# Softmax sums of two 16-head attentions as accumulator outputs of the exponentials

## The chip, the cores and the metric

The kernel runs on one core of a Trainium2 chip. The metric is the device time of one execution in microseconds (us), measured on that core. Engines are named as in the profile: PE is TensorE (matmuls and transposes, with its weight loads as PEld), DVE is VectorE, ACT is ScalarE, POOL is GpSimd, SP is SyncE, which issues the DMAs. Each engine works through its own queue of instructions in order; semaphores hold an instruction until others have finished.

## What is computed

The reference is a chain of four layers on x (2 x 1024 tokens, 256 wide) with a context of 77 tokens. Each layer adds an attention to the context and then a feed-forward. The change touches the attentions of layers 0 and 1, which have the same form (cut from the reference):

```python
q, k, v = heads(layernorm(x) @ Wq), heads(ctx @ Wk), heads(ctx @ Wv)   # 16 heads of 16
scores = q @ k.T / 4                       # 1024 x 77 for each head
scores = where(mask, -huge, scores)
attn = softmax(scores, axis=-1)            # exp(s - max) / sum(exp(s - max))
x = x + (attn @ v) @ Wo + bo
```

The feed-forward of layer 0 is a mixture of 8 experts with all experts computed and two gated; layer 1's is an 8-bit quantized product; layer 2 has a one-head attention and a mixture of experts, layer 3 an attention with rotary embedding and a routed mixture of experts.

## The kernel before

The 2048 tokens are four groups (g) of 512; a group is four tiles (j) of 128 tokens, so an attention has 16 iterations `it = 4 g + j`. `attention(...)` (L296) is used for layer 0 (`layer0_attention`, L482) and layer 1 (`layer1_attention`, L557). It first makes the keys (`kblk`) and values (`vblk`) as block matrices, and then runs a hand-written pipeline (`pipelined`, L246): at each step `ahead` (layer norm, transposing and queries of the next group: `prepare`, `queries`), `scores(it)`, two empty stages, `values` two tiles at a time, and for layer 1 the stage `beside`, which places the pieces of layer 1's feed-forward and layer 2's attention (`quantized`, L593, to `add`, L682) beside the attention.

`scores(it)` works in two chunks c of 8 heads each, so an attention has 32 chunks:

- PE writes the mask into PSUM (L394, two matmuls with an identity of bf16) and adds the scores of 8 heads (L401), in a PSUM tile of two banks from a pool of two (`pbig`); the scores have the opposite sign.
- For each half of four heads (i = 0, 1) DVE takes the four minima (L410, which are the maxima with the sign turned), and ACT makes four exponentials, one for each head, 128 rows by 77 keys, with the minimum as bias (L412). They go to the SBUF tile s.
- DVE sums s over the keys, eight heads in one instruction (L417, 616 elements a row), and takes the reciprocal (L418). POOL multiplies the chunk by it (L419).

`values(it)` transposes two tiles' weights on PE (L437), copies them out of PSUM on ACT (L443) or DVE (L445), multiplies with the values (L450), copies on ACT (L455), multiplies with Wo (L459), and DVE adds the result to x (L464).

The queries are made at L374 and leave PSUM on ACT (L379 or L383); the transposed tokens at L175 leave it on ACT (L179) and DVE (L181). The exponential of layer 3's attention is at L981, with sums at L985, which are not touched. L1002 is a copy from PSUM on ACT in layer 3.

The program is built with `tile.TileContext(nc, schedule_with_timeline_sim=True)` (L1489): a scheduler sets the order in which each engine's instructions stand, from the program text, the dependencies and the buffers of the pools. So an edit in `scores` can also reorder instructions around it. The small tile sm comes from a pool entry of four buffers ("smc"), the minima from one of six ("mxc").

POOL also has one all-reduce over partitions, L580, for layer 1's quantized weights, which the scheduler places among the first scalings of layer 0.

Of the kernel before, what the change touches and what calls it, by code (L numbers as in the profile page):

```python
# [22 lines left out]
F32 = mybir.dt.float32  # L23
# [5 lines left out]
ALU = mybir.AluOpType  # L29
AX = mybir.AxisListType  # L30
# [3 lines left out]
P = 128  # L34
# [32 lines left out]
def tile_layers(ctx: ExitStack, tc: tile.TileContext, a: dict, out: bass.AP):  # L67
    nc = tc.nc
# [5 lines left out]
    st = ctx.enter_context(tc.tile_pool(name="st", bufs=3))  # L74
# [6 lines left out]
    def pbig(name):  # L81
        return ps2.tile([P, 2, 512], F32, tag="p2", name=name)
# [148 lines left out]
    def bc(v, n):  # L231

        return v.unsqueeze(len(v.shape)).to_broadcast([*v.shape, n])
# [62 lines left out]
    def attention(lay, weights, mask, deep=5, beside=None):  # L296
# [4 lines left out]
        with tc.tile_pool(name=f"at_{lay}", bufs=2) as ap:  # L301
# [84 lines left out]
            def scores(it):  # L386
                g, j = divmod(it, J)
                n = f"{lay}{g}{j}"
                s = ap.tile([P, 2, 8, L], F32, tag="s", name=f"s_{n}", bufs=deep)
                for c in range(KC):  # L390

                    sc = pbig(f"psc_{n}{c}")[:, :, : 4 * L]
                    for i in range(2):
                        nc.tensor.matmul(  # L394
                            sc[:, i].rearrange("p (h k) -> p h k", k=L), identb,
                            mb[:, g, j, :].unsqueeze(1).to_broadcast([P, 4, L]),
                            start=True, stop=False,
                        )
                    for i in range(2):
                        rows = slice(64 * i, 64 * i + 64)  # L400
                        nc.tensor.matmul(  # L401
                            sc[:, i], qTs[g][rows, c, j * P : (j + 1) * P],
                            kblk[g // 2][rows, c, 4 * i : 4 * i + 4, :]
                            .rearrange("p h k -> p (h k)"),
                            start=False, stop=True,
                        )
                    for i in range(2):
                        sv = sc[:, i].rearrange("p (h k) -> p h k", k=L)
                        mx = st.tile([P, 4], F32, tag="mxc", name=f"mx_{n}{c}{i}", bufs=6)
                        nc.vector.tensor_reduce(mx, sv, AX.X, ALU.min)  # L410
                        for h in range(4):
                            nc.scalar.activation(  # L412
                                s[:, c, 4 * i + h, :], sv[:, h, :], AF.Exp,
                                bias=mx[:, h : h + 1], scale=-1.0,
                            )
                    sm = st.tile([P, 8], F32, tag="smc", name=f"sm_{n}{c}", bufs=4)
                    nc.vector.tensor_reduce(sm, s[:, c], AX.X, ALU.add)  # L417
                    nc.vector.reciprocal(sm, sm)  # L418
                    nc.gpsimd.tensor_tensor(s[:, c], s[:, c], bc(sm, L), ALU.mult)  # L419
                ss[it] = s  # L420
# [49 lines left out]
            def ahead(it):  # L470

                g, j = divmod(it, J)
                if g + 1 < G and j < 3:
                    begin[j](g + 1)

            stages = [ahead, scores, lambda it: None, lambda it: None, values]
            if beside:
                stages.append(beside)
# [1014 lines left out]
```

## Time and profile before

| what | value |
|---|---|
| median of 3 timed runs | 1148.5 us (1147.95 to 1149.76) |
| the profiled execution | 1150.59 us |
| its span, first to last instruction | 1148.7 us |
| mean granted PE clock in it | 0.952 |
| busy: PE, DVE, ACT, POOL | 1029.8, 719.4, 362.1, 386.3 us |
| exponentials L412, both attentions | 512, 337 ns each, 121.5 us |
| sums L417 | 64, 785 ns each, 50.3 us |
| reciprocals L418 | 64, 191 ns each, 12.2 us |
| scalings L419 on POOL | 64, 1223 ns each, 78.3 us |

The profile's page shows one execution. Its first part gives busy time by engine, its second the span in 40 slices of 28.7 us with the busy share in tenths. The chain of work that ended last is followed back from the last instruction, at each step to what released it; its shares say on which engine and line the time was spent that nothing else hid. A group of instructions is given with its line, engine, operation, tiles (out<-in), shapes and count, then busy us and mean ns of one, then the idle time of the engine just before them and who ended it. Busy time can be asked for in chosen stretches: then a line holds the stretch, its length, the busy us (with instructions) of PE, PEld, DVE, ACT and POOL, the granted PE clock, the DMA share and GB/s. The exponentials of layer 0 run from 28 to some 159 us, those of layer 1 from some 313 to 436 us.

### The profile page before, as it was taken

The numbers are of one execution on the slowest core, as the hardware profiler recorded it, in microseconds if no ns is written. First come the engines' busy times: TensorE is split into PE (matmuls) and PEld (weight loads), VectorE is DVE, ScalarE is ACT, GpSimd is POOL, SyncE is SP. The second block draws the span as 40 slices with busy tenths as digits, with TensorE's granted clock in tenths as the row PEclk, the third lists the DMA queues.
The fourth block names the chain that finished last, engine by engine and source line by source line (L and its number), as shares of the span: only waits on it lengthen the run. The fifth ranks groups of instructions, "written<-read, shape, count | busy, mean of one in ns | idle before, by whom it ended". The sixth has DMA issues, their size and how long they took to land.

```text
span 1148.7 us, 13916 instructions
## 1 busy us (share of the span) xinstructions
PE 1029.8 (90%) x4770; PEld 645.5 (56%) x4770; DVE 719.4 (63%) x1848; ACT 362.1 (32%) x1115; POOL 386.3 (34%) x368
## 2 busy tenths in 40 slices
PE   5499999999998987897998999899899958999996
PEld 3255554444444444455655546577678844766774
DVE  5567965776578898949586547677878731222211
ACT  1457640000076563131231110555355521111100
POOL 5443320112343544423120000675566641121211
PEclk9699998999999898898999999999999987999998
DMA  8400008245200000111102004523042323253630
GB/s 269 57 3 1 1 23 165 38 82 88 80 1 1 1 1 1 39 48 31 40 23 59 1 1 161 145 45 67 23 103 51 90 83 96 77 165 101 200 131 17
DMA packets 100279, 74.89 MB, mean 65 GB/s; under 512 B 57916, under 2 KB 90476, under 8 KB 100206
## 3 DMA queue, kind: packets, MB, share of 16 engines
q1 hardware_dynamic: 92974, 58.20, 18.3%
q10 hardware_dynamic: 4800, 9.46, 4.8%
q0 software_dynamic: 2432, 6.31, 1.6%
q8 instruction: 40, 0.66, 0.2%
q14 instruction: 33, 0.27, 0.1%
HBM read 55.35 MB, written 19.64 MB: 65 GB/s over the span
## 4 chain that ended last, share of the span: by engine, by line
PE 56%; DVE 24%; DMA 7%; ACT 4%; issue 4%; POOL 4%; SPq 0%; POOLq 0%; DVEq 0%; ACTq 0%
PE pe_f L545 10%; PE pgu_f L745 8%; PE poe_e L1273 4%; PE ph_e L1253 4%; PE po_a L1007 4%; DMA out_x<-ye_e,ids_e 3%; PE pq_a L930 3%; DVE x L765 3%; PE pc_a L450 3%; DVE x L156 2%; PE po_f L758 2%; PE pPT_a L437 2%; DVE mx_a L410 2%; DMA xe_e<-buf 2%; DVE sm_a L417 2%
## 5 line engine op out<-in xcount | busy, mean ns | idle before, releaser
L412 ACT ACTIVATE s_a<-psc_a,mx_a 128x77 f32<-128x77 f32 x512 | 121.5, 337 | 58.5 <-DVE mx_a L410 52.1
L419 POOL TENSOR_TENSOR s_a<-s_a,sm_a 128x616 f32<-128x616 f32 x64 | 78.3, 1223 | 123.9 <-DVE sm_a L418 89.4
L545 PE MATMUL pe_f<-ew,xnT_f 128*128 128x512 f32 x256 | 117.1, 607 | 0.0
L551 DVE SCALAR_TENSOR_TENSOR x<-pe_f,gate_f,x 128x256 f32<-128x256 f32 x128 | 61.8, 483 | 43.3 <-PE pe_f L545 40.7
L981 ACT ACTIVATE s_a<-s_a,mx_a 128x77 f32<-128x77 f32 x256 | 67.2, 347 | 61.4 <-DVE mx_a L979 61.2
L545 PEld LDWEIGHTS pe_f<-ew,xnT_f 128*128 128x128 f32 x256 | 48.3, 195 | 55.0 <-issue 53.0
L1007 PE MATMUL po_a<-vw,PT_a 128*128 128x256 f32 (+1 forms) x320 | 77.3, 381 | 0.8 <-ACT PT_a L1002 0.8
L1253 PE MATMUL ph_e<-xT_e,w 128*128 128x320 f32 x256 | 75.6, 436 | 0.0
L758 PE MATMUL po_f<-down2T,hT_f 128*128 128x256 f32 x256 | 65.0, 400 | 8.8 <-DVE x L765 8.7
L437 PE MATMUL pPT_a<-cst,s_a 128*128 128x128 f32 (+1 forms) x320 | 55.0, 292 | 17.8 <-POOL vr_a L343 11.5
L410 DVE TENSOR_REDUCE mx_a<-psc_a 128x4 f32<-128x308 f32 x128 | 57.9, 466 | 18.6 <-PE psc_a L401 11.4
L1077 DVE TENSOR_SCALAR hT_e<-ph_e,b1c 128x320 f32<-128x320 f32 (+1 forms) x36 | 20.6, 572 | 75.3 <-PE ph_e L1253 75.3
L930 PE MATMUL pq_a<-wq,xnT_a 128*128 128x512 f32 x128 | 60.5, 610 | 4.7 <-DVE s_a L972 4.7
L745 PE MATMUL pgu_f<-xnT_f,gate2T 128*128 128x512 f32 x128 | 63.5, 619 | 1.0 <-DVE hT_f L751 0.6
L765 DVE SCALAR_TENSOR_TENSOR x<-po_f,cw_f,x 128x256 f32<-128x256 f32 x128 | 60.8, 480 | 5.7 <-PE po_f L758 2.5
L437 PEld LDWEIGHTS pPT_a<-cst,s_a 128*128 128x128 f32 (+1 forms) x320 | 35.9, 143 | 49.5 <-issue 17.9
L1007 PEld LDWEIGHTS po_a<-vw,PT_a 128*128 128x128 f32 (+1 forms) x320 | 57.8, 190 | 9.6 <-issue 1.4
L1075 ACT ACTIVATE hT_e<-ph_e,b1c 128x320 f32<-128x320 f32 (+1 forms) x36 | 19.6, 545 | 138.0 <-PE ph_e L1253 138.0
L1273 PE MATMUL poe_e<-w,hT_e 128*128 128x256 f32 x256 | 61.3, 381 | 0.0
L758 PEld LDWEIGHTS po_f<-down2T,hT_f 128*128 128x128 f32 x256 | 48.3, 197 | 22.7 <-DVE x L765 15.4
L450 PE MATMUL pc_a<-PT_a,vblk_a 128*32 128x256 f32 (+1 forms) x512 | 57.2, 400 | 4.2 <-DVE PT_a L445 2.2
L745 PE MATMUL pgu_f<-xnT_f,up2T 128*128 128x512 f32 x128 | 60.1, 592 | 0.0
(311 smaller groups left out, 1979.8 us busy)
## 6 DMA issues: line engine op xcount, KB each, us to landing
w<-in_L_ffn_w SPq DMA_DIRECT2D x16, 1024.0 KB
rb_a<-in_relbias SPq DMA_DIRECT2D x16, 616.0 KB
buf<-none ACTq DMA_DIRECT2D x12, 769.5 KB
vd<-vo SPq DMA_DIRECT2D x8, 308.0 KB
vw<-vd SPq DMA_DIRECT2D x2, 1152.0 KB
xe_e<-buf SPq DMA_DIRECT2D x8, 257.0 KB
x<-in_x SPq DMA_DIRECT2D x4, 512.0 KB
ew<-in_L_ffn_expert_w SPq DMA_DIRECT2D x4, 512.0 KB
```

The costliest lines, as they stand in the source:

```text
L410: nc.vector.tensor_reduce(mx, sv, AX.X, ALU.min)
L412: nc.scalar.activation(s[:, c, 4 * i + h, :], sv[:, h, :], AF.Exp, bias=mx[:, h : h + 1], scale=-1.0,)
L437: nc.tensor.transpose(pt[: wide(m), m - m0, k * P : (k + 1) * P], sp[k][:, c, m * P : m * P + wide(m)], ident,)
L450: nc.tensor.matmul(pc[cols, c, :], vblk[g // 2][: wide(m), c, m, cols], t[: wide(m), m, :], start=(k == 0), stop=(k == 1),)
L545: nc.tensor.matmul(pe[:, i, :], xnT[:, kc, j * P : (j + 1) * P], ew[half][:, kc, i * 512 : (i + 1) * 512], start=(kc == 0), stop=(kc == KC ...
L745: nc.tensor.matmul(pgu[:, i, :], wgu[i][:, kc, e * INTER : (e + 1) * INTER], xnTs[g][:, kc, :], start=(kc == 0), stop=(kc == KC - 1),)
L758: nc.tensor.matmul(po[:, e // 2, (e % 2) * D : (e % 2) * D + D], hTs[g, half][:, e, j * P : (j + 1) * P], wd[:, 4 * half + e, :], start=Tr ...
L765: nc.vector.scalar_tensor_tensor(x, po[:, e // 2, (e % 2) * D : (e % 2) * D + D], cws[g][:, j, ee : ee + 1], x, ALU.mult, ALU.add,)
L930: nc.tensor.matmul(pq[:, i, :], xnTs[g][:, kc, j * P : (j + 1) * P], wq[:, kc, i * 512 : (i + 1) * 512], start=(kc == 0), stop=(kc == KC - 1),
L1007: nc.tensor.matmul(po, t[:w, m, :], vws[g // 2][:w, m, :], start=(m == 0), stop=(m == NC3 - 1))
L1253: nc.tensor.matmul(ph[:, h % 2, :rows], w1[:, kc, h * P : (h + 1) * P], xT[:, kc, :], start=(kc == 0), stop=(kc == KC - 1),)
L1273: nc.tensor.matmul(po, hT[:, h, i * P : (i + 1) * P], w2[:, h, :], start=(h == 0), stop=(h == NH - 1),)
```

## The change

The tile sm is taken before the exponentials. Each exponential writes the sum of its 77 results into one column of sm as its accumulator output. The DVE sum of the chunk is gone; the reciprocal and the scaling stay. Layer 3's softmax and layer 2's stay as they are. In the changed file the lines of this function from the minimum to the exponential stand one lower (L411, L413); L418 and L419 keep their numbers.

```diff
                         start=False, stop=True,
                     )
+                sm = st.tile([P, 8], F32, tag="smc", name=f"sm_{n}{c}", bufs=4)
                 for i in range(2):
                     sv = sc[:, i].rearrange("p (h k) -> p h k", k=L)
                     mx = st.tile([P, 4], F32, tag="mxc", name=f"mx_{n}{c}{i}", bufs=6)
                     nc.vector.tensor_reduce(mx, sv, AX.X, ALU.min)
                     for h in range(4):
                         nc.scalar.activation(
                             s[:, c, 4 * i + h, :], sv[:, h, :], AF.Exp,
                             bias=mx[:, h : h + 1], scale=-1.0,
+                            accum_out=sm[:, 4 * i + h : 4 * i + h + 1],
                         )
-                sm = st.tile([P, 8], F32, tag="smc", name=f"sm_{n}{c}", bufs=4)
-                nc.vector.tensor_reduce(sm, s[:, c], AX.X, ALU.add)
                 nc.vector.reciprocal(sm, sm)
                 nc.gpsimd.tensor_tensor(s[:, c], s[:, c], bc(sm, L), ALU.mult)
```

## The prediction

> **What bounds the kernel now.** I read the page's engine shares and its chain of work that ended last, then the chain again stretch by stretch, then the engines' busy time in the same stretches, and last the groups of instructions with their shapes.
>
> ```profile
> PE 1029.8 (90%) x4770; PEld 645.5 (56%) x4770; DVE 719.4 (63%) x1848; ACT 362.1 (32%) x1115; POOL 386.3 (34%) x368
> ...
> DVE  5567965776578898949586547677878731222211
> ACT  1457640000076563131231110555355521111100
> ...
> PE 56%; DVE 24%; DMA 7%; ACT 4%; issue 4%; POOL 4%; SPq 0%; POOLq 0%; DVEq 0%; ACTq 0%
> ```
>
> ACT is 32% busy as a mean, but nearly all of that lies in slices 2 to 6 and 12 to 16 and in layer 3: the mean says nothing about the two attentions that change. In those slices DVE has its eights and nines too. So the question is asked of five stretches: two of layer 0's attention (57-112, 112-157 us), three of layer 1's.
>
> ```profile
> 57.00:112.00 55.00, 54.59 (x334) 29.14 (x335) 38.52 (x88) 36.18 (x131) 22.74 (x21) 0.95 0.02 2
> 112.00:157.00 45.00, 43.83 (x314) 24.97 (x314) 43.60 (x132) 29.27 (x115) 17.23 (x16) 1.00 0.03 5
> 316.00:352.00 36.00, 33.82 (x207) 17.14 (x207) 25.67 (x59) 26.64 (x104) 15.31 (x12) 1.00 0.00 1
> 352.00:391.00 39.00, 33.37 (x202) 17.82 (x201) 34.51 (x89) 24.09 (x91) 16.93 (x18) 0.87 0.01 1
> 391.00:449.00 58.00, 47.56 (x332) 28.07 (x331) 55.08 (x139) 31.81 (x111) 30.34 (x28) 1.00 0.00 1
> ```
>
> The columns after the length are PE, PEld, DVE, ACT, POOL. DVE is nearly full in the second (43.6 of 45) and the last (55.1 of 58); the chain of these two runs through DVE almost without a break. In 57-112 the chain is PE alone, matmul after matmul. In 316-352 it passes through 32 exponentials on ACT.
>
> **The change, part by part.**
>
> ```profile
> L412 ACT ACTIVATE s_a<-psc_a,mx_a 128x77 f32<-128x77 f32 x512 | 121.5, 337 | 58.5 <-DVE mx_a L410 52.1 <-DVE s_a L665 1.8 <-PE pPT_a L437 1.3
> L417 DVE TENSOR_REDUCE sm_a<-s_a 128x8 f32<-128x616 f32 x64 | 50.3, 785 | 10.5 <-ACT s_a L412 9.9
> L1002 ACT COPY PT_a<-pPT_a 128x512 f32<-128x512 f32 x32 | 18.0, 581 | 14.8 <-PE pPT_a L1000 14.8
> L1002 ACT COPY PT_a<-pPT_a 128x128 f32<-128x128 f32 x16 | 4.3, 266 | 2.5 <-PE pPT_a L1000 2.4
> ```
>
> *Removed:* 64 sums on DVE (L417), 50.3 us busy. What counts is how much of that is on the chain. Pieces "DVE sm_a L417" of the chain add up to 2.2 us in 24-57, none in 57-112, 7.9 in 112-157, 1.5 in 316-352, 2.9 in 352-391 and 7.0 in 391-449: 21.5 us, the "DVE sm_a L417 2%" of the page. A sample, where each piece is the 0.70 us by which the next VectorE instruction is held up:
>
> ```profile
> 128.26 0.70 DVE sm_a L417
> 128.96 0.77 DVE mx_a L410 x2
> 129.73 0.12 DVE sm_a L418
> 129.85 0.06 issue
> 129.91 0.56 ACT s_a L412 x2
> 130.47 0.02 issue
> 130.49 0.80 DVE sm_a L417
> ```
>
> *Added:* 512 accumulator outputs, one to each exponential, on ACT. The trace has none, so the price x of one is bounded. Below: 0, if the sum rides along. Above: a separate read-out that overlaps nothing. The two L1002 copies give (581-266)/384 = 0.82 ns a column, so an ACT instruction of one column would be about 266-105 = 160 ns. Four exponentials in a row take 0.97 us ("106.22 0.97 ACT L412 ... x4" of the timeline), so the pitch is (970-337)/3 = 211 ns and each overlaps its neighbour by 126. A read-out that overlaps on both sides adds 160-126 = 34 ns; one that waits for its exponential's end and overlaps only with the next adds 160; one without any overlap adds 160+126 = 286. **x is 0 to 0.286; I take 0.10**, midway between the first two: a read-out of one column is nearest to a small instruction in an overlapping row, and what speaks against its full overlap is that the sum is complete only with the last column. The trace can't decide it, and it is the weak step.
>
> The Trainium skill, "ScalarE: Activation LUTs", section "What ACT_TABLE_LOAD costs", puts an ACTIVATE with immediates at 186 ns + 0.833 ns a column, a pointer bias at 93 more, and the overlap of neighbours at 93. Its 344 ns for our exponential is near the row's 337; its overlap is under the row's 126. An estimate for one column by it is 187-93 = 94 ns, and the sum below would come out 0.4 us lower with that. The same page's "Rules for kernel authors" speaks against the change: additions belong on VectorE. It prices no accumulator output; the row it would defend is L417, 785 ns for eight sums against eight read-outs.
>
> What x does to ACT's room: idle time of ACT in a stretch over its exponentials there is 18.8/110 = 0.171 us in 57-112, 15.7/99 = 0.159 in 112-157, 9.4/92 = 0.102 in 316-352, 14.9/78 = 0.191 in 352-391, 26.2/85 = 0.308 in 391-449. At x = 0.10 ACT just fits everywhere. Besides, each exponential on the chain costs x there: 2 in 112-157, 32 in 316-352, 23 in 352-391, 13 in 391-449.
>
> *Moved and new waits:* the reciprocal (L418) now waits for ACT directly. In the changed order of DVE it stands between the two maxima (L411) of the next chunk, so the second maximum is queued behind it; it is covered by the four exponentials of the first maximum, 0.97+4x us, as long as ACT isn't behind. The tile sm is taken before the exponentials, so the first of them waits for the POOL scaling (L419) of four chunks earlier. Behind it on ACT stand the copies that PE needs (L443, L455). At the measured pace a chunk takes about 3.6 us and scaling follows the reciprocal at once (POOL is idle 89.4 us waiting for L418), so this wait is met some 10 us early. It bites once: the second chunk is scaled only at 52.52, and the sixth chunk's exponentials (49.6 now) wait for that till about 53.7; PE stands still until 57.4 anyway. Cost 0; where POOL got stuck later it would be ACT's stall. The order of PE and DVE after the attentions (from layer 2's feed-forward on) is the same as before, no DMA is added or moved, and the PE order inside the attentions changes only by a few transposes against scores. Order alone: 0, within 3 us either way.
>
> *Start, 24-57 us.* Here the chain follows POOL: scaling at 34.66, 7.06 us idle, the all-reduce of L580, 7.63 idle, scaling again at 52.52, and PE waits 11.5 us for what follows. The first scaling waits for the reciprocal at 34.32, which was queued behind a sum (33.06) and a maximum. In the changed order it comes right after the copy L181 that ends at 33.0, and the exponentials (32.06, four more of pitch 0.31) end near 33.3: POOL starts at about 33.6. -1.0 us.
>
> *The sum at x = 0.10*, against the profiled execution's 1150.6 us (span 1148.7):
> - 24-57: -1.0.
> - 57-112: 0. No sum is on the chain; PE goes on.
> - 112-157: 7.9 leaves, but PE is late next. Its instructions there at their pitches on the chain (48 L401 at 0.18, 24 L394 at 0.135, 112 L450 at 0.097, 65 L437 at 0.135, 24 L459 at 0.216, L194 and L175 4) need 41 of the 45 us. -4.1, and 2 exponentials +0.2: -3.9.
> - 316-352: -1.5 + 32 x 0.10 = +1.7.
> - 352-391: -2.9 + 23 x 0.10 = -0.6.
> - 391-449: -7.0 + 13 x 0.10 = -5.7. PE needs about 44 of 58 us here and isn't next.
>
> Together -9.5: 1141.1 us. The three timed runs have their median at 1148.5, 2.1 under the profiled one, so a timed median may lie near 1139. I say 1140. With x = 0 the same sum is -17 (1133); its own range, with 2 us for order, is 1132 to 1148.
>
> **Rivals.**
>
> *Slower: ACT becomes the bound.* One mechanism, the price of a read-out. Past its room in a stretch, ACT's need (busy plus count times x) sets the length. At x = 0.20: 36.2+22.0 = 58.2 in 57-112 (+3.2), 49.1 in 112-157 (+4.1), 45.0 in 316-352 (+9.0), +1.7 and -4.4 by the chain in the other two: +13.6, 1164 us. At 0.286: +12.7, +12.6, +16.9, +7.4, -3.3 = +46 and some 2 at the ends: 1198. It decides from x = 0.16, where the sum is near 0 (+5.3 in 316-352 against -4.9 in the last). For it: ACT's room in 316-352 is only 0.102, and the read-out depends on its exponential's end. Against: neighbours on ACT overlap by 126 ns already.
>
> *Nothing measurable.* x near 0.15 (gain and loss meet), or PE takes the place of DVE in 391-449 as in 112-157, and the sums come back as waits of DVE for ACT: 1147 to 1152. For it: PE is 48 of 58 busy there by its records.
>
> *The sums were hidden.* If the chain overrates them and only the DVE-full stretches give half, with x = 0.10: -1.0-2-3+1.7 = -4, 1146. This is still faster, and part of the first case.
>
> **How the numbers follow.** x under 0.14 with DVE's relief arriving: 0.56, predicted 1140. x of 0.14 to 0.17 or gains eaten by PE: 0.09. x over 0.17, ACT the bound: 0.35, at 1164 if in the middle. Within 0.2% (2.3 us) is about what this kernel's measurement can't tell from no change, so faster 0.56, same 0.09, slower 0.35. The range takes in both bounds of x: 1131 to 1200; the likeliest case's own is 1132 to 1148.
>
> **What would show it.** A row of L413 on ACT, or a second ACT row beside it, gives x: four in a row should take about 1.3 us (0.97 now). DVE's busy time should fall by about 50 us and ACT's rise by about 50 (146 would be the upper bound). DVE should be under 40 of its 45 us in the stretch that ends layer 0's attention, and the chain there should name PE. The start of the transposes, now at 57.4 us, should come 1 us earlier. The prediction is wrong if the chain of the attentions names ACT L413 over long stretches, or if DVE idles before L418 waiting for ACT while PE waits for scores.

## The result and the profile after

The changed kernel takes 1154.87 us (median of 13 runs, 1151.03 to 1158.01); the kernel before took 1149.76 on the same chip (13 runs, 1145.83 to 1151.99). The ratio is 1.0047, 95% interval 1.0035 to 1.0059: **slower** by 0.47%, where 1140 and faster was forecast. The profiled execution has a span of 1152.4 us (1148.7 before) at a granted clock of 0.959 (0.952).

First the page of the changed kernel: busy time, two rows of the 40 slices, and the chain's shares by engine.

```profile
PE 1030.5 (89%) x4770; PEld 645.1 (56%) x4770; DVE 680.3 (59%) x1784; ACT 404.8 (35%) x1627; POOL 386.8 (34%) x368
...
DVE  6446755776546788868687446677877741222211
ACT  1488760000088774222231110454355521111110
...
PE 57%; DVE 20%; DMA 7%; ACT 6%; issue 4%; POOL 3%; SPq 1%; POOLq 0%; DVEq 0%; ACTq 0%
```

The work moved as meant: DVE is 39.1 us less busy, ACT 42.7 more. On the chain DVE lost 4 points, ACT won 2, PE 1. So the relief reached DVE, and yet the end came later. The groups of the attentions in the changed kernel (busy, mean ns, then idle time before them and who ended it):

```profile
L413 ACT ACTIVATE s_a<-psc_a,mx_a 128x77 f32<-128x77 f32 x512 | 159.1, 340 | 46.9 <-DVE mx_a L411 44.5
...
L413 ACT ACTIVATION_READ_ACCUMULATOR s_a<-psc_a,mx_a 128x1 f32 x512 | 113.0, 221 | 0.0
...
L411 DVE TENSOR_REDUCE mx_a<-psc_a 128x4 f32<-128x308 f32 x128 | 57.2, 469 | 28.2 <-ACT s_a L413 24.3
```

The read-out is an instruction of its own, one to each exponential, and never waits (0.0). Its 221 ns are not its price, since it overlaps on both sides. The order in time on ACT shows the price (start, length):

```profile
104.62 0.33 ACT L413 ACTIVATE s_a<-psc_a,mx_a 128x77 f32<-128x77 f32 x1
104.85 0.19 ACT L413 ACTIVATION_READ_ACCUMULATOR s_a<-psc_a,mx_a 128x1 f32 x1
104.94 0.32 ACT L413 ACTIVATE s_a<-psc_a,mx_a 128x77 f32<-128x77 f32 x1
105.15 0.20 ACT L413 ACTIVATION_READ_ACCUMULATOR s_a<-psc_a,mx_a 128x1 f32 x1
105.24 0.32 ACT L413 ACTIVATE s_a<-psc_a,mx_a 128x77 f32<-128x77 f32 x1
```

From one exponential to the next it is now 0.300 us (104.94 to 105.24); before it was 0.211. **x = 0.089 us**, and four take 1.3 us, as forecast. 512 x 0.089 = 45.6 us fits ACT's 42.7. (The Trainium skill, "ScalarE: Activation LUTs", section "What ACT_TABLE_LOAD costs", gave 94 ns as an estimate for a one-column instruction. The rise of 89 ns is within 5 ns of it, but the read-out's own row, 221 ns, is longer than the 187 ns that the estimate starts from, so part of the agreement is luck.)

The five stretches of the forecast (length; PE, PEld, DVE, ACT, POOL busy; clock; DMA):

```profile
57.00:112.00 55.00, 54.61 (x345) 29.96 (x346) 29.16 (x75) 45.21 (x240) 21.01 (x19) 0.97 0.02 2
112.00:157.00 45.00, 41.29 (x281) 22.66 (x281) 33.23 (x111) 34.35 (x197) 16.42 (x16) 1.00 0.00 1
316.00:352.00 36.00, 32.34 (x190) 16.24 (x189) 18.60 (x49) 30.50 (x168) 14.38 (x12) 1.00 0.07 27
352.00:391.00 39.00, 34.26 (x227) 17.35 (x225) 28.16 (x82) 31.41 (x173) 18.73 (x19) 1.00 0.01 1
391.00:449.00 58.00, 50.58 (x338) 29.84 (x338) 47.38 (x135) 42.90 (x225) 26.05 (x27) 0.97 0.00 1
```

No engine is full except PE in the first. DVE's idle time over the five grew from 35.6 us to 76.5: by 40.9. The waits of the changed kernel say where it went (engine and tile, whom it waited for, us, times, longest):

```profile
ACT s_a L413 <- DVE mx_a L411: 44.5, 43, 4.9
DVE sm_a L418 <- ACT s_a L413: 31.9, 35, 1.8
DVE mx_a L411 <- ACT s_a L413: 24.3, 30, 1.5
...
PE psc_a L394 <- ACT s_a L413: 7.2, 13, 1.1
```

The second and third line, 56.2 us, were 16.3 in the kernel before, with the sum (L417) where the reciprocal waits now:

```profile
DVE sm_a L417 <- ACT s_a L412: 9.9, 15, 1.1
...
DVE mx_a L410 <- ACT s_a L412: 6.4, 10, 1.0
```

That is 39.9 us more. **As a sum, DVE's relief became waiting for ACT.** What such waiting costs is another question, and the first experiment shows that it isn't read from the sum. ACT meanwhile still waits 44.5 us for DVE's minima (52.1 before). The two wait for each other in turn.

A piece of the chain at the end of layer 1's attention shows such a turn (start, us, what):

```profile
429.70 1.35 ACT s_a L413 x8
431.05 0.02 issue
431.08 0.20 DVE sm_a L418
431.28 0.55 DVE x L464
431.83 0.60 DVE xnT_a L181
432.43 0.66 DVE bns_f L147 x2
433.09 0.39 DVE mx_a L411
433.48 0.02 issue
433.51 1.34 ACT s_a L413 x8
434.85 0.02 issue
434.87 0.20 DVE sm_a L418
```

Four exponentials with their read-outs (x8), then the reciprocal that had stood waiting at the head of DVE's queue, behind it the residual, a copy, the statistics and a minimum, then ACT, which meanwhile had made four more exponentials and a copy and then idled 0.76 us for that minimum, and the reciprocal again. DVE had idled 0.94 us before the first of the two reciprocals and 0.88 us before the second.

Two marks are used below beside the whole time: layer 0's end (its last expert matmul) and layer 3's start (its first query matmul), both in the profiled execution. Before: 310.1 and 709.0; changed: 314.2 and 713.3. So all the loss, 4.3 us, lies ahead of layer 3, and 4.1 of it in layer 0. A mark comes from one execution, which lay up to 4.1 us from its kernel's median (e7 and e8), and it moves with the granted clock too; a table at the end of the experiments puts the marks and the clock side by side.

### The profile page after: what moved, and what is told of

It is laid out like the page before. It is cut to its first block, busy times and chain, and to the rows that moved or that the text cites. A ratio compares the mean times of both kernels' runs of the same rounds, so it can differ in the third digit from the quotient of the medians.

```text
span 1152.4 us, 14352 instructions
## 1 busy us (share of the span) xinstructions
PE 1030.5 (89%) x4770; PEld 645.1 (56%) x4770; DVE 680.3 (59%) x1784; ACT 404.8 (35%) x1627; POOL 386.8 (34%) x368
## 4 chain that ended last, share of the span: by engine, by line
PE 57%; DVE 20%; DMA 7%; ACT 6%; issue 4%; POOL 3%; SPq 1%; POOLq 0%; DVEq 0%; ACTq 0%
PE pe_f L545 10%; PE pgu_f L745 8%; PE poe_e L1273 4%; PE po_a L1007 4%; PE ph_e L1253 4%; ACT s_a L413 3%; DMA out_x<-ye_e,ids_e 3%; PE pc_a L450 3%; PE pq_a L930 3%; DVE x L765 3%; PE pPT_a L437 2%; PE po_f L758 2%; DMA xe_e<-buf 2%; DVE x L156 2%; PE psc_a L965 2%
## 5 line engine op out<-in xcount | busy, mean ns | idle before, releaser
L413 ACT ACTIVATE s_a<-psc_a,mx_a 128x77 f32<-128x77 f32 x512 | 159.1, 340 | 46.9 <-DVE mx_a L411 44.5
L419 POOL TENSOR_TENSOR s_a<-s_a,sm_a 128x616 f32<-128x616 f32 x64 | 78.0, 1219 | 125.5 <-DVE sm_a L418 97.4
L413 ACT ACTIVATION_READ_ACCUMULATOR s_a<-psc_a,mx_a 128x1 f32 x512 | 113.0, 221 | 0.0
L411 DVE TENSOR_REDUCE mx_a<-psc_a 128x4 f32<-128x308 f32 x128 | 57.2, 469 | 28.2 <-ACT s_a L413 24.3
L437 PEld LDWEIGHTS pPT_a<-cst,s_a 128*128 128x128 f32 (+1 forms) x320 | 35.6, 142 | 54.0 <-issue 20.9
L745 PE MATMUL pgu_f<-xnT_f,gate2T 128*128 128x512 f32 x128 | 61.0, 598 | 1.2 <-DVE hT_f L751 0.6
```

The source lines that it names most:

```text
L413: nc.scalar.activation(s[:, c, 4 * i + h, :], sv[:, h, :], AF.Exp, bias=mx[:, h : h + 1], scale=-1.0, accum_out=sm[:, 4 * i + h : 4 * i + ...
L437: nc.tensor.transpose(pt[: wide(m), m - m0, k * P : (k + 1) * P], sp[k][:, c, m * P : m * P + wide(m)], ident,)
L745: nc.tensor.matmul(pgu[:, i, :], wgu[i][:, kc, e * INTER : (e + 1) * INTER], xnTs[g][:, kc, :], start=(kc == 0), stop=(kc == KC - 1),)
```

## The experiments

The theories at the outset: **A**, ACT's throughput is the bound. **H**, the handshake within a chunk: in both kernels the second minimum of a chunk stands behind the four exponentials of the first half (in all 64 chunks of both traces it starts after them); the forecast had not seen this wait. Both halves lie in one PSUM tile; that this is the reason was not tested apart. **R**, the reciprocal stands at the head of DVE's in-order queue until ACT has finished the chunk.

The edits are shown shortened. Each ratio is against the kernel before on the same chip, where its median was 1148.8 to 1152.2 us; the ratios, not the microseconds, can be compared from one experiment to another.

### What the relief and the read-outs are worth alone

**e1_no_sum**: the kernel before without the sum; the weights are scaled by a value made from one key of each head, so they are no softmax. Layer 3's routing turns out different by this, so only the time to layer 3's start is read.

```diff
-tensor_reduce(sm, s[:, c], AX.X, ALU.add)
-reciprocal(sm, sm)
+tensor_scalar(sm, s[:, c, :, 0], -0.5, 1.0, ALU.mult, ALU.add)
```

> Exponentials as before, without accumulator output; the sum over keys is left out (a small VectorE operation on one key of each head, 8 elements a row, stands where the reciprocal was, and still waits for the last exponential of the chunk). This is the gain side of the change alone. Theory H (handshake: the second maximum of a chunk waits for the four exponentials of the first, so a longer exponential stretches a chain that VectorE's relief can't shorten): 5 to 12 us faster than before, 1138 to 1145, since here the exponentials are not longer. Theory R (the operation that now waits for ScalarE at the head of VectorE's queue costs what the sums gave): no gain, 1147 to 1152, as the wait is here too. Theory O (another order by the scheduler is what cost): nothing certain, within 5 us of before.

Whole: 1224.75 us, ratio 1.0622, with one more pass of layer 3's experts in it. Layer 3 starts at 693.8, **15.2 us earlier** than before. The forecast's sum without a price for the read-outs was -17 (its terms add up to -16.5): the relief is real and near the forecast. 4.2 us of it lie in layer 0; the other 11.0 come with a higher granted clock in layer 1's attention (0.99 against 0.96 from 310 to 450 us), and how much of them is the clock was not measured. Both expectations missed: H said 5 to 12 us, R no gain, because the operation that stands for the reciprocal waits for ACT here too. It does:

```profile
DVE mx_a L410 <- ACT s_a L412: 22.1, 27, 1.6
...
DVE sm_a L417 <- ACT s_a L412: 14.6, 22, 1.2
```

DVE waits 36.7 us for ACT here, more than twice the 16.3 before, in a kernel that is 15.2 us ahead. So neither the sum of the waits nor a wait at the head of DVE's queue is a cost by itself.

**e2_price_only**: the changed kernel with its read-outs, and the DVE sum put back.

```diff
+tensor_reduce(sm, s[:, c], AX.X, ALU.add)
 reciprocal(sm, sm)
```

> Accumulator outputs as in the changed kernel, and the VectorE sum kept as well (it writes the same sums over them). This is the cost side alone: 512 read-outs at a pitch of 0.09 us. H: the chunk's chain gets longer by two times 0.36 us and nothing is given back: 12 to 25 us slower than before, 1162 to 1175. R: about as the changed kernel, 1152 to 1158, because the sum waits where the reciprocal waits. If ScalarE had room, as the prediction had it: within 3 us of before.

1156.16 us, ratio 1.0036 (1.0020 to 1.0052); layer 3 starts at 715.9, 6.9 later than before. H's 12 to 25 us missed, R's "about as the changed kernel" held. So with the sums on DVE the read-outs cost 6.9, and without them (e1 against the changed kernel) 19.5. And with the read-outs there, taking the sums away brings 2.6 us at this mark and nothing that the whole time resolves (1.0036 against 1.0047). The two don't add: DVE's time seems to be worth little once ACT is slower.

### The second minimum's wait

**e3_one_max_acc** and **e4_one_max_sum**: one minimum instruction over all eight heads, in the changed kernel and in the kernel before. The wait within the chunk is gone.

```diff
-for i in range(2):
-    mx = st.tile([P, 4], ...); tensor_reduce(mx, sc[:, i], AX.X, ALU.min)
+mx = st.tile([P, 2, 4], ...); tensor_reduce(mx, sc, AX.X, ALU.min)
```

> The changed kernel, with one maximum for the 8 heads of a chunk instead of two for 4 heads each, so that no maximum waits for exponentials of its own chunk. H: 8 to 20 us faster than the changed kernel, 1135 to 1147, and the read-outs no longer leave ScalarE idle between the halves (44.5 us idle for the maxima now, under 25 then). R: as the changed kernel, 1150 to 1158, since the reciprocal waits as it did.

> The kernel before, with one maximum for the 8 heads of a chunk. Separates what the single maximum is worth by itself from what it is worth to the change. H: it helps before too, by less (its fours are 0.97 us, not 1.33): 2 to 10 us faster than before, 1140 to 1148, and the change on top of it is a gain. R: within 4 us of before, and the change on top of it a loss as it was.

e3: 1148.28 us, ratio 0.9946 (0.9923 to 0.9969). e4: 1137.5, ratio **0.9871** (0.9847 to 0.9895), the fastest of all. Layer 3 starts at 704.4 and 694.0. So the single minimum is worth much in both kernels (e4 gains more than the 2 to 10 us that H said). But with it the change still costs 10.4 us at layer 3's start, where H expected a gain. H explains a loss that was there before, not the one that the change made. The waits that remain in e3:

```profile
DVE sm_a L418 <- ACT s_a L413: 28.7, 24, 2.6
...
ACT s_a L413 <- DVE mx_a L410: 16.8, 15, 3.1
...
PE psc_a L394 <- ACT s_a L413: 14.1, 14, 4.3
```

ACT's wait for minima fell from 44.5 to 16.8; DVE's wait before the reciprocal hardly moved.

**e6_two_first_sum** and **e7_two_first_acc**: still two minima, but both issued ahead of the chunk's eight exponentials.

```diff
-for i in range(2): minimum(i); four exponentials(i)
+for i in range(2): minimum(i)
+for i in range(2): four exponentials(i)
```

> The kernel before, with both maxima of a chunk taken ahead of its eight exponentials: the same two VectorE instructions, but the second one no longer waits for ScalarE. It tells whether the gain of the single maximum (15 us) was the wait or the VectorE time saved (64 x some 0.1 us). H: 8 to 15 us faster than before, 1137 to 1144. If it was the VectorE time: within 4 us of before.

> The changed kernel with both maxima ahead of the eight exponentials. H: 4 to 9 us faster than the changed kernel, about 1146 to 1151, as with the single maximum. A: ScalarE stays the bound, so it is 8 to 13 us slower than the same kernel with VectorE sums; if VectorE's relief counted, it would be faster than that one.

e6: 1143.21 us, 0.9948 (0.9929 to 0.9967). e7: 1144.22, 0.9953 (0.9937 to 0.9968). DVE does here what it did before, in another order, and gains, though in the whole less than H's 8 to 15 us and less than e4. In layer 0 it gains as much as e4: it ends at 298.5 (e4 299.8, before 310.1). There it was the wait, not the instruction. e6 falls behind e4 in layer 1's attention, where its granted clock is 0.91 against 0.96. The change on top of it (e7) costs 5.9 us in layer 0, 3.1 at layer 3's start (705.7 against 702.6) and nothing that the whole time resolves; A's 8 to 13 us are not there.

### ACT's throughput

**e8_copies_dve**: the changed kernel with all copies of the transposed weights on DVE, which unloads ACT.

```diff
-if m0 == 0 or m0 == 4 and c == 0:
+if False:
     scalar.copy(...)
```

> The changed kernel, with the copies of the transposed weights out of PSUM (three of five were on ScalarE: 32 of 593 ns and 16 of 386) all on VectorE, which has the time that its sums left. A: ScalarE gets about 20 us of its 45 us of read-outs back, so 6 to 12 us faster than the changed kernel, 1143 to 1149. H or R alone: these copies fill gaps in which ScalarE waits anyway, and VectorE gets longer: within 3 us of the changed kernel or slower.

1153.75 us, 1.0051 (1.0033 to 1.0070), layer 3 starts at 711.0, 2.3 before the changed kernel: no gain in the whole, where A said 6 to 12 us. A falls.

### The reciprocal

**e5_recip_pool**: the changed kernel, with the reciprocal as a power of -1 on POOL. **e11_pool_idle_recip**: the same, with an idle reciprocal of four minima a chunk put back on DVE, which waits for nothing on ACT. **e10_sum_recip_pool**: the control, the kernel before with its reciprocal on POOL.

```diff
-nc.vector.reciprocal(sm, sm)
+nc.gpsimd.tensor_tensor(sm, sm, negone, ALU.pow)
```

```diff
 nc.vector.tensor_reduce(mx[:, :4], sv, AX.X, ALU.min)
+if i == 0:
+    nc.vector.reciprocal(mx[:, 4:], mx[:, :4])
```

> The changed kernel, with the reciprocal of the eight sums made on POOL (a power of -1, some 1.1 us by the row of the like power of -0.5, 64 times), so that nothing on VectorE waits for the last exponentials of a chunk. Theory R (the reciprocal at the head of VectorE's queue, 31.9 us of waits before it, is what cost): at least 6 us faster than the changed kernel, 1149 or less. Theory A (ScalarE is the bound of the attentions once the read-outs are there, and VectorE's waits are only its idle time): within 3 us of the changed kernel, 1152 to 1158.

> The changed kernel with the reciprocal on POOL, and beside it an idle reciprocal of four minima per chunk on VectorE, whose result nothing uses and which waits for nothing on ScalarE: VectorE's time is back, the wait is not. If the wait was the cost: as with the reciprocal on POOL alone, 0.993 to 0.998 of the kernel before. If VectorE's time was: back near the changed kernel, 1.002 to 1.006.

> Control: the kernel before, sums on VectorE, with only the reciprocal on POOL. The reciprocal there waits for VectorE's own sum, not for ScalarE; the sum itself waits for ScalarE and stays on VectorE. If the gain of the reciprocal's move in the changed kernel was the wait taken from VectorE's queue, this one gains little: within 3 us of the kernel before (0.997 to 1.003). If it was VectorE's 12 us of reciprocals (64 of 0.19 us), it gains here as there, 5 to 11 us (0.990 to 0.996).

e5: 1143.74 us, 0.9953 (0.9937 to 0.9968). e11: 1150.56, 0.9983 (0.9964 to 1.0002), between the two expectations and nearer to the first. e10: 1155.17, 1.0021 (1.0008 to 1.0035): no gain in the whole. Layer 3 starts at 703.9, 704.5 and 713.5. One small instruction moved takes 9 us from the changed kernel and nothing from the one before, and giving DVE its time back costs 0.6 of them at that point (some 3 by the whole times). The granted clock has a part in the control: from 310 to 450 us it is 0.90 in e10, 0.96 before. Layer 0, where the clocks are alike, is the better place to compare: the move gains 6.1 us there in the changed kernel (e5, 314.2 to 308.1), 4.7 in e11 and 1.2 in the kernel before. That speaks for R.

**e9_one_max_acc_pool** and **e12_one_max_sum_pool**: one minimum of eight heads and the reciprocal on POOL together (both edits above).

> The changed kernel without either wait of VectorE for ScalarE: one instruction takes the minima of all eight heads, and POOL takes the reciprocal (power -1). If the change lost its gain to these two waits (second minimum behind four exponentials; reciprocal at the head of VectorE's queue), both gains should come together: one minimum alone gave 0.9946 of the kernel before, the reciprocal on POOL alone 0.9953, so some 0.990 and at least as fast as the kernel with one minimum and sums on VectorE (0.9871) less 3 us, with idle time of DVE for ACT in the attentions under 10 us. If read-outs on ScalarE are themselves the bound, it stays near 0.995.

> The kernel before with one instruction for the minima of eight heads, and the reciprocal on POOL; the sums stay on VectorE. One minimum alone gave 0.9871. If only waits of VectorE for ScalarE count, the reciprocal's move adds nothing here: 0.985 to 0.989. If VectorE's time counts in its full stretches, it gains another 3 to 6 us: 0.981 to 0.985.

e9: 1154.16 us, 1.0020 (1.0008 to 1.0033); e12: 1154.33, 1.0013 (0.9998 to 1.0028). Both missed by far: the two gains don't add. Rows of e9:

```profile
L421 POOL TENSOR_TENSOR sm_a<-sm_a,powers 128x8 f32<-128x8 f32 x64 | 106.6, 1667 | 24.4 <-ACT s_a L416 15.5 <-issue 7.0 <-PE pPT_a L440 1.7
```

```profile
DVE mx_a L413 <- PE psc_a L404: 49.3, 34, 9.4
...
ACT s_a L416 <- POOL s_a L422: 16.5, 2, 12.7
...
PE psc_a L397 <- ACT s_a L416: 14.2, 12, 3.9
```

A power of 8 columns takes 1.67 us on POOL, more than the scaling of 616 (1.22). A chunk needs 2.9 us there, in e5, e10 and e11 too. In e9 ACT waits for POOL, in one place for 12.7 us: POOL has become a limit, so these two can't tell R from its rivals. Besides, e9 took 9 us more than the changed kernel from layer 2's feed-forward (457.7) to layer 3's start, at a granted clock of 0.91 in 470-700 us against 0.96: the same 210 us of PE busy time held 724 matmuls there and 755 in the changed kernel. Why that clock was lower there, no run tells.

### The reciprocal without POOL

**e13_recip_after**: the reciprocal stays on DVE, but is bound behind the next chunk's second minimum: this minimum is written into four more columns of the sums' tile, and the reciprocal takes all twelve into another tile, of which the scaling uses eight.

```diff
+rs.append(st.tile([P, 12], ...)); sm = rs[t]
 for i in range(2):
-    mx = st.tile([P, 4], ...)
+    mx = rs[t - 1][:, 8:] if i == 1 and t else st.tile([P, 4], ...)
...
-nc.vector.reciprocal(sm, sm)
-nc.gpsimd.tensor_tensor(s[:, c], s[:, c], bc(sm, L), ALU.mult)
+nc.vector.reciprocal(inv, rs[t - 1])
+nc.gpsimd.tensor_tensor(s_before, s_before, bc(inv[:, :8], L), ALU.mult)
```

**e15_recip_after_idle_sum**: e13, with a sum over eight heads put back on DVE behind that reciprocal, used by nothing. **e14_one_max_recip_after**: e13's edit with one minimum of eight heads, the reciprocal bound behind the minimum of two chunks later.

> The changed kernel, with the reciprocal of a chunk bound behind the next chunk's second minimum: these four minima are written beside the eight sums, and the reciprocal takes all twelve columns into a tile of its own, of which the scaling uses eight. It stays on VectorE, and POOL has nothing more to do. Before it stands a minimum that itself waits for four later exponentials, so the reciprocal should never wait for ScalarE. If the wait at the head of VectorE's queue took the gain: idle time before the reciprocal under 3 us (31.9 in the changed kernel), layer 0 ends 4 to 8 us earlier than in the changed kernel (314.2), and the time is 0.992 to 0.998 of the kernel before. If the second minimum's own wait for ScalarE takes over what the reciprocal gives up, or the longer exponentials are the cost in themselves: that wait (24.3 us) grows by as much, and the time stays at 1.002 to 1.006.

> As the kernel with the reciprocal behind the next chunk's second minimum, and one sum over eight heads a chunk put back on VectorE behind that reciprocal, whose result nothing uses: 64 of 0.79 us, 50 us of VectorE's time, without a new wait for ScalarE. If the relief of VectorE is worth something once the wait is away, this is 7 to 17 us slower than that kernel (the prediction's sum without the price of a read-out was 17). If VectorE's time was never what counted, within 3 us of it.

> The changed kernel with one minimum of eight heads, and the reciprocal bound behind the minimum of two chunks later, on VectorE: neither wait, and no work moved to POOL. The kernel with one minimum and the accumulated sums stood at 0.9946, and the same with sums on VectorE at 0.9871. If the waits of VectorE for ScalarE are all that the change costs, this one comes to the latter or below it (0.980 to 0.988). If the read-outs on ScalarE cost by themselves, by making PE wait for the PSUM tile, it stays at 0.992 to 0.997.

The three ran on one chip. e13: 1143.56 us, **0.9960** (0.9944 to 0.9977). e15: 1160.33, 1.0110 (1.0088 to 1.0132). e14: 1137.23, 0.9912 (0.9891 to 0.9932). Layer 0 ends at 308.1 in e13 (314.2 changed, 310.1 before), layer 3 starts at 702.8, 718.9 and 696.6. The waits of e13 (sm_a L424 is the second minimum, inv_a the reciprocal):

```profile
DVE sm_a L424 <- ACT s_a L426: 33.7, 29, 2.4
ACT s_a L426 <- DVE mx_a L424: 25.5, 19, 4.3
...
ACT s_a L426 <- DVE sm_a L424: 15.1, 22, 1.6
...
DVE inv_a L365 <- ACT s_a L426: 6.6, 7, 1.5
```

The reciprocal's wait fell from 31.9 to 6.6 us (under 3 was expected); the second minimum's grew from 24.3 to 33.7, so a part was passed on, as the rival had it, but the sum fell from 56.2 to 40.3, and the change is now a gain of 0.4% in place of a loss of 0.5%. By e15, with the reciprocal out of the way DVE's 50 us of sums are worth 16.8 us (1160.33 - 1143.56), near the forecast's 17; with the reciprocal in the way they were worth 2.6 (e2). Two things weaken this: the scaling waits for e15's sum too, which reads the weights that the scaling overwrites, and 4.4 of the 16.1 us by layer 3's start come after layer 1's attention, where no sums stand, at a granted clock of 0.93 against 0.96 (450 to 700 us). And e15 is slower than e2, 718.9 against 715.9, though in e2 the sum waits 19.3 us for ACT at the head of DVE's queue. Where the sums stay on DVE, moving the reciprocal gains nothing.

What the read-outs cost by themselves is small and not resolved. With one minimum and the reciprocal out of the way the change costs 2.6 us at layer 3's start (e14 against e4, 696.6 and 694.0), nothing in layer 0 (299.1 and 299.8), and 0.4% in the whole with intervals that just overlap. In e14 PE waits for the PSUM tile twice as long as in e4 (7.0):

```profile
PE psc_a L402 <- ACT s_a L426: 14.9, 18, 4.0
```

Beyond both kernels: e4 (0.9871) and e14 (0.9912). The version to keep is e4, one minimum and sums on DVE.

The marks of the profiled executions (us), and the granted PE clock from 310 to 450 us, which is most of layer 1's attention. From 24 to 310 us the clock is 0.94 to 0.96 in all of them, so layer 0's end is the fairer mark.

| kernel | layer 0 ends | layer 3 starts | clock, 310 to 450 |
|---|---|---|---|
| before | 310.1 | 709.0 | 0.96 |
| changed | 314.2 | 713.3 | 0.99 |
| e1, no sum, no read-out | 305.9 | 693.8 | 0.99 |
| e2, sum and read-out | 312.4 | 715.9 | 0.94 |
| e4 and e3, one minimum: sum, read-out | 299.8, 305.6 | 694.0, 704.4 | 0.96, 0.95 |
| e6 and e7, two minima first: sum, read-out | 298.5, 304.4 | 702.6, 705.7 | 0.91, 0.96 |
| e5 and e11, changed, reciprocal on POOL | 308.1, 309.5 | 703.9, 704.5 | 0.98, 0.99 |
| e10, before, reciprocal on POOL | 308.9 | 713.5 | 0.90 |
| e13, changed, reciprocal behind | 308.1 | 702.8 | 0.96 |
| e14, e3, reciprocal behind | 299.1 | 696.6 | 0.96 |
| e15, e13 with a sum | 313.9 | 718.9 | 0.96 |

In layer 0 the change costs 4 to 6 us wherever the reciprocal waits for ACT (4.1, e3 against e4 5.8, e7 against e6 5.9), and it gains 0.6 to 2.1 us where it doesn't (e5, e11 and e13 against before; e14 against e4 0.7).

## Why the prediction was wrong, point by point

**The price of a read-out** was right: 0.10 taken, 0.089 measured. Four in a row take 1.3 us, ACT's busy time rose by 43 us of the 50 forecast.

**The relief of DVE** was near in size. Forecast -17 at no price; e1 gives -15.2, e15 against e13 16.8, both with an unknown part of the granted clock in them. DVE's busy time fell by 39, not 50: a part of this is that the sums' rows of 785 ns overlap their neighbours (a piece of the chain is 0.70 us).

**The read-outs on the path** were near in size: 7.0 us in the sum (70 exponentials at 0.10), and 9.0 measured from e1 to e13 at layer 3's start (693.8 to 702.8; 2.2 of it in layer 0). But their place was wrong. "Each exponential on the chain costs x there" counted 70 exponentials, those of the chain before. The changed kernel's chain at layer 1's start shows the real form:

```profile
320.51 2.47 ACT s_a L413 x16
322.98 0.02 issue
323.01 0.49 DVE mx_a L411
323.50 0.02 issue
323.52 2.57 ACT s_a L413 x16
```

Eight exponentials with read-outs (the second half of one chunk and the first of the next), the minimum that waits for them, eight again: 3.0 us a chunk on the chain, without a gap. The eight take 2.5 us, where they took 1.83 before. ACT and DVE's minimum take turns here.

**The failed step** stands under "Moved and new waits": the reciprocal "now waits for ACT directly", and the minimum behind it was held to be "covered by the four exponentials of the first maximum, 0.97+4x us, as long as ACT isn't behind". The sum has no term for this wait. It cost some **10 us**: 1.0047 against 0.9960 of the kernel before with and without it (e13), 713.3 against 702.8 at layer 3's start, and there 9.4 and 8.8 by e5 and e11. The condition failed in 35 of the 64 chunks, where DVE stood idle before the reciprocal, 31.9 us in all. The piece of the chain at 429.70 shows how: the second minimum of a chunk comes only after four exponentials, so ACT is still at the second half when DVE gets to the reciprocal; the read-outs move that half's end back, and DVE idles while work for PE and ACT stands behind the reciprocal. The forecast named this very sign ("if DVE idles before L418 waiting for ACT") and gave it no price.

The terms now, as steps from before to e1, to e13 and to the changed kernel: -15.2 + 9.0 + 10.5 = +4.3 at layer 3's start, and in layer 0 alone -4.2 + 2.2 + 6.1 = +4.1. Steps from kernel to kernel must add up; that the last one is the reciprocal's wait rests on e13, e5 and e11, which take it away in two different ways. The first two are less clean: e1's operation waits for ACT as well, and the granted clock from 310 to 450 us goes from 0.96 to 0.99 and back to 0.96. In the last step it rises to 0.99, so the clock doesn't make this loss.

**"At x = 0.10 ACT just fits everywhere"** is where it came from. The room was idle time divided by exponentials. But much of ACT's idle time was waiting for minima (52.1 us), and the second minimum of each chunk itself waits for ACT. With 42.7 us more work on ACT this idle time shrank by only 7.6, to 44.5: most of it wasn't room. The wait DVE mx_a <- ACT, 6.4 us in the profile before, was the hint, and it wasn't read.

**The smaller points.** The transposes start 0.38 us earlier (57.03 against 57.41), not 1.0. The chain of 112-157 should have named PE; its first line is ACT L413, 24.2%, with PE's largest, L459, at 8.5%. The buffers of sm cost nothing, as said: the waits of the changed kernel list none of these exponentials for POOL.

**The rivals.** "ACT becomes the bound" had the sign and the wrong mechanism: it should decide from x = 0.16, and the kernel lost at 0.089, with ACT full in none of the five stretches (at most 30.5 of 36 us); e8 shows that its load isn't the point. "Nothing measurable" had the mechanism in half a sentence, the sums coming back "as waits of DVE for ACT" (1147 to 1152), and the smallest chance.

**What stays open.** The chain shows the reciprocal's wait handed on in single places (0.94 and 0.88 us at the end of layer 1's attention). No view adds these places up to 10 us. Nor is it shown why such a wait costs nothing visible in e1, which has no read-outs, and why taking it away gains nothing where the sums stay on DVE (e15 against e2): the 10 us hold for the changed kernel, not for every wait at the head of a queue. Each edit also moves other instructions in the scheduler's order, and the granted clock of a stage moves with the edit; how much of a difference of 2 or 3 us between two kernels is either, was not measured.

## What to carry to other kernels

When work goes from one engine to another, look for a pair of engines that wait for each other in turn: there the idle time of either is not simply room. A small instruction that must wait for another engine can cost what is queued behind it; try it behind an instruction that waits longer anyway (in the changed kernel worth 0.9% for 64 instructions of 0.2 us). A total of waits doesn't give the price: only the run without the wait does. Take from the waits, before pricing an edit, which waits run in both directions between the two engines: removing that one (a single minimum, 1.3%) was worth more than the edit itself.

## What the runs showed of the hardware

- An accumulator output of an exponential appears as a second ACT row, ACTIVATION_READ_ACCUMULATOR, 221 ns as a mean (0.19 to 0.33), which overlaps so far that it adds 0.089 us to a 128x77 exponential's 0.211.
- Eight sums over 77 keys are one DVE row of 785 ns, or 8 x 89 = 712 ns more on ACT. In busy time the move took 39.1 us from DVE and gave 42.7 to ACT: on this shape the accumulator saves nothing as a sum over both engines.
- On POOL a power of 128x8 takes 1.67 us, the same reciprocal on DVE 0.197.
